# Two token tiles' row sums and norms moved ahead of the first tile's biases on VectorE, in the opening of layer 0's attention

## The chip, the cores and the metric

The kernel runs on one core of a Trainium2 chip. A core has TensorE for matmuls (PE in the profile; its weight loads are PEld), VectorE (DVE), ScalarE (ACT), GpSimd (POOL) and SyncE (SP), which mostly issues DMAs. The engines run their own instruction lists in order and wait for each other by semaphores. The metric is the device time of one launch in microseconds; times in this document are microseconds, counted from the start of the profiled span.

## The reference

Two transformer layers in half-step ("macaron") form on 1024 tokens of width 512, all in float32:

```python
x = L0_attn_hidden_states                      # (1, 1024, 512)
x = x + 0.5 * L0_ffn(layernorm(x))             # 16 experts, top 4, and a shared expert
x = x + L0_attn(layernorm(x))                  # 32 query heads, 8 key/value heads of 16, RoPE, causal
x = x + 0.5 * L0_ffn(layernorm(x))
x = x + 0.5 * L1_ffn(layernorm(x))             # permuted, 16 heads, GELU
x = x + L1_attn(layernorm(x))
x = x + 0.5 * L1_ffn(layernorm(x))
```

The expert layer and the attention, cut to what matters here:

```python
out = einsum('eti,ehi->th', silu(x @ Wg.T) * (x @ Wu.T) * cw, Wd)   # routed part, 4 of 16 experts
out = out + silu(x @ Sg.T) * (x @ Su.T) @ Sd.T                      # shared expert

qkv = einsum('bsh,oh->bso', x, w_qkv) + b_qkv
q, k = rope(q), rope(k)
probs = softmax(where(mask, q @ k.T / 16, min))
out = (probs @ v) @ w_dense.T + b_dense
```

The mask is causal at this length: each query sees all keys up to its own place.

## The kernel before, in words

The 1024 tokens lie in eight tiles of 128 rows. `x_sb` holds all of them in on-chip memory for the whole kernel, one row a partition. The stages follow each other: routing and experts of layer 0, its attention, the same expert layer again, then layer 1.

The expert stage writes its rows, sorted by expert, to a table `y_d` in DRAM. Each token has four rows there. The attention's opening brings them back, and finishes the shared expert for tiles 4 to 7, while it already prepares the first tiles for the scores. The steps of the opening, by the names in the code:

- `moe.fetch(t)` (L869) issues four indirect gathers on GpSimd's queue, which bring the four rows of each token of tile t into buffers `yk`, of which there are eight, for two tiles. `moe.add(t)` (L877) adds them to `x_sb` with four VectorE additions of 128x512.
- `norm_a(t)` (L927) takes the statistics on VectorE (`bn_stats`, `bn_aggr`, an epsilon added) and the power -0.5 on GpSimd (`norm_stats`, L283). `norm_b(t)` (L930) makes the normed rows `xn` with one VectorE instruction.
- `turn(t)` (L933) turns `xn` with four TensorE transposes, and ScalarE copies the result to `xT`.
- `z20` to `z31` (the hidden part of the shared expert) are matmuls with `wsh`, an activation and a VectorE product. `y4` to `y7` (`shared_y`, L524) are the output of the shared expert for tiles 4 to 7: four matmul instructions each, and one VectorE instruction that adds half of it to `x_sb`.
- `project_q(t)` (L943) and `project_kv(t)` (L951) are eight matmul instructions each with `wqkv_sb`, followed by VectorE additions of the bias `bqkv_sb`: one of 128x512 for the queries, two of 128x128 for keys and values.
- `rope_a(t)` and `rope_b(t)` (L966, L976) rotate queries and keys with four VectorE instructions for tiles 0 to 2 and write `aug`. `turn_k` and `turn_q` (L983, L996) turn `aug` with ten TensorE transposes, and ScalarE copies them to `kT` and `qt`.
- `maxima(t, i)` (L1193) computes scores only to find each row's maximum: masks and products on TensorE, four reductions on VectorE. `max_done(t)` (L1056) turns the maxima `nm` and sends them with four SyncE DMAs into a spare row of `qt`, so that the later score matmuls subtract them.
- `moe.collect((4, 5), k)` (L881) issues gathers on GpSimd's queue that add rows of tiles 4 and 5 to `x_sb` in flight. `mid()` loads the shared expert's weights for the second expert layer.

The order is written out by hand. Matmuls are pinned in program order (`pin`, L69). VectorE and GpSimd work goes through a wrapper that ties each instruction to the one before it on that engine (`Ordered`, L89), so the order of the calls at L1201 to L1245 is the order on these engines, within each. All matmul results lie in eight banks of matmul memory that are handed out in turn (`bank`, L123). A bank is written again when its reader is done.

After L1245 a loop over the eight tiles mixes the scores of tile t, the maxima of tile t+1 and the projections of tile t+2.

## Time and profile before

| | us |
|---|---|
| runs, median (lowest to highest of 3) | 1266.63 (1263.77 to 1272.97) |
| the profiled execution | 1270.88 |
| its span from first to last instruction | 1269.2 |

Busy time of the engines in five stretches of the profiled span, with the clock granted to TensorE as a share of full speed:

| stretch, us | what runs | TensorE busy | VectorE busy | clock |
|---|---|---|---|---|
| 290 to 340 | opening of the attention | 42.10 of 50 | 28.74 | 0.93 |
| 340 to 380 | scores of the first tiles | 32.56 of 40 | 21.34 | 0.79 |
| 380 to 700 | the rest of the attention | 313.72 of 320 | 206.62 | 0.98 |
| 700 to 1046 | routing and experts again | 321.81 of 346 | 78.84 | 0.96 |
| 1046 to 1269 | layer 1 | 174.75 of 223 | 106.36 | 0.87 |

How to read the lines of such a profile. A timeline line has the start, the time that the instruction or the group took, the engine, the line of the code (often that of a helper: L82 is every matmul, L85 every transpose, L99 everything that goes through the ordering wrapper), the operation, what is written and read, the shape and the count. In brackets is the time that the engine stood idle before it, and whose end released it. A line of the windows has the window, its length, the busy time of TensorE, its weight loads, VectorE, ScalarE and GpSimd, each with the number of instructions, and then the granted clock, the share of the DMA engines and GB/s.

### The profile page before, as it was taken

Reading aid. Unit: us, or ns where it says so; the run is one execution under the profiler, and the core shown is the slowest. Engines: PE = TensorE matmul, PEld = TensorE weight load, DVE = VectorE, ACT = ScalarE, POOL = GpSimd, SP = SyncE. Lnnn points to the kernel's source line nnn. Section 1 sums busy time; section 2 is a strip of 40 time slices with the busy share of each in tenths; the row PEclk is TensorE's granted clock in tenths of the full one; section 3 lists DMA queues with packets and bytes.
Section 4 is the critical chain, followed back from the end, with each engine's and each line's share of the span. In section 5 each row is a group of like instructions: output and inputs, shape, how many; then the busy total and the mean of one; then the engine's idle time right before and its main releaser. Section 6 shows DMA issues by size and latency. Waiting matters only on the chain. (4 is left out here: it accounts for less than half of the span.)

```text
span 1269.2 us, 18211 instructions
## 1 busy us (share of the span) xinstructions
PE 1158.0 (91%) x6230; PEld 528.4 (42%) x6230; DVE 511.4 (40%) x1172; ACT 451.3 (36%) x868; POOL 307.6 (24%) x377
## 2 busy tenths in 40 slices
PE   8899999997889999999989997899998997697886
PEld 6543333335534444444333335444333336354432
DVE  4711111114566674656587206341111115645631
ACT  4312222221245535363555683112221221431543
POOL 5201112104345522021101010411111107552032
PEclk7999999999979999899989998899999998877998
DMA  6545467524422200000000003546247515630034
GB/s 233 183 158 175 150 215 273 168 92 120 114 34 35 43 1 10 1 10 9 10 1 10 10 1 108 207 153 202 89 142 273 175 52 156 185 122 3 21 119 159
DMA packets 49329, 133.87 MB, mean 105 GB/s; under 512 B 6496, under 2 KB 13408, under 8 KB 45136
## 3 DMA queue, kind: packets, MB, share of 16 engines
q1 hardware_dynamic: 22112, 63.10, 14.4%
q0 software_dynamic: 15152, 47.53, 13.4%
q10 hardware_dynamic: 11968, 22.02, 4.6%
q8 instruction: 52, 0.85, 0.3%
q14 instruction: 45, 0.37, 0.1%
HBM read 276.15 MB, written 34.08 MB: 244 GB/s over the span
## 5 line engine op out<-in xcount | busy, mean ns | idle before, releaser
L82 PE MATMUL ps<-wg,xsT 128*64 128x512 f32 x1120 | 263.3, 612 | 8.5 <-DMA wg<-in_w_exp_dram 6.7
L99 DVE TENSOR_REDUCE nm<-ps 128x1 f32<-128x512 f32 (+5 forms) x360 | 195.2, 599 | 78.3 <-PE ps L82 77.8
L82 PE MATMUL ps<-kT,qt 32*128 32x512 f32 (+3 forms) x768 | 168.8, 536 | 3.5 <-DVE nm L99 3.2
L1098 ACT ACTIVATE pt<-ps 128x512 f32<-128x512 f32 x224 | 119.3, 602 | 126.5 <-PE ps L82 126.1
L82 PE MATMUL ps<-qt,kT 32*128 32x512 f32 x576 | 155.0, 652 | 1.6 <-DMA qt<-nmT 1.1
L747 POOL DMA_INDIRECT xs<-xn_d,src_i x70 | 68.0, 972 | 358.8 <-PE ps L85 316.8
L82 PEld LDWEIGHTS ps<-wg,xsT 128*64 128x64 f32 x1120 | 76.7, 140 | 145.4 <-issue 141.0
L82 PE MATMUL ps<-wd,zT 128*64 128x512 f32 x560 | 133.3, 593 | 1.0 <-DVE zT L99 1.0
L99 DVE TENSOR_TENSOR z<-sg,ps 128x256 f32<-128x256 f32 x70 | 29.4, 421 | 249.5 <-ACT sg L99 249.5
L99 ACT ACTIVATE sg<-ps 128x256 f32<-128x256 f32 x70 | 26.8, 384 | 259.4 <-PE ps L82 259.4
L808 ACT ACTIVATE y<-ps,w_row 128x512 f32<-128x512 f32 x70 | 48.1, 687 | 105.5 <-PE ps L82 56.6
L99 POOL TENSOR_TENSOR rstd<-rstd,mhalf 128x1 f32<-128x1 f32 x48 | 28.7, 599 | 229.3 <-DVE rstd L99 225.0
L82 PEld LDWEIGHTS ps<-kT,qt 32*128 32x128 f32 x768 | 63.7, 187 | 45.1 <-DVE nm L99 14.9
L99 POOL TENSOR_SCALAR_AFFINE_SELECT pt<-pt 128x512 f32<-128x512 f32 x64 | 41.1, 653 | 165.0 <-ACT pt L1102 154.2
L82 PE MATMUL ps<-pt,va 128*32 128x512 f32 x576 | 80.4, 624 | 0.0
L99 POOL DMA_INDIRECT yk<-y_d,row_i x48 | 50.5, 1052 | 95.4 <-SPq L859 82.4
L82 PEld LDWEIGHTS ps<-wd,zT 128*64 128x64 f32 x560 | 40.8, 137 | 78.8 <-issue 77.3
L82 PEld LDWEIGHTS ps<-qt,kT 32*128 32x128 f32 x576 | 49.9, 188 | 54.3 <-issue 27.1
L99 DVE COPY zT<-ps 128x256 f32<-128x256 f32 x70 | 29.6, 423 | 102.6 <-PE ps L85 102.5
L82 PE MATMUL ps<-xT,wsh 128*128 128x256 f32 x256 | 62.8, 402 | 4.8 <-PEq L859 2.6
L85 PE MATMUL ps<-ident,xn 128*128 128x128 f32 x192 | 35.9, 318 | 33.7 <-DVE xn L99 28.1
L82 PEld LDWEIGHTS ps<-xT,wsh 128*128 128x128 f32 x256 | 50.2, 201 | 15.2 <-ACTq L859 6.6
(238 smaller groups left out, 1413.8 us busy)
## 6 DMA issues: line engine op xcount, KB each, us to landing
wg<-in_w_exp_dram SPq DMA_DIRECT2D x142, 1024.0 KB
wd<-in_w_exp_dram SPq DMA_DIRECT2D x142, 512.0 KB
y_d<-y ACTq DMA_DIRECT2D x70, 256.0 KB
xn_d<-xn SPq DMA_DIRECT2D x16, 256.0 KB
wsh<-in_w_exp_dram SPq DMA_DIRECT2D x2, 1536.0 KB
xd<-xT SPq DMA_DIRECT2D x12, 256.0 KB
y_d<-y ACTq DMA_DIRECT2D x2, 1280.0 KB
out_dram<-xo SPq DMA_DIRECT2D x8, 256.0 KB
```

The lines of the kernel that those rows point to most:

```text
L82: pin(nc.tensor.matmul(dst, lhsT=lhsT, rhs=rhs, start=start, stop=stop))
L85: pin(nc.tensor.transpose(dst, src, ident))
L99: ins = f(*a, **k)
L747: nc.gpsimd.indirect_dma_start(out=xs, out_offset=None, in_=self.xn_d, in_offset=bass.IndirectOffsetOnAxis(ap=self.src_i[:, s : s + 1], ax ...
L808: nc.scalar.activation(y, py, AF.Copy, scale=self.w_row[:, s : s + 1])
L1098: nc.scalar.activation(pt, pas[j], AF.Exp, scale=1.0 / 16.0)
```

## The change

In the hand-written order of the opening, four calls of tile 1 and two of tile 2 stand elsewhere. `moe.add(1)` and `norm_a(1)` come ahead of `y4()` and `project_q(0)`; `norm_b(1)` comes ahead of `project_kv(0)` and the rotation of tile 0; `turn(1)` comes ahead of `y5()`; `moe.add(2)` and `norm_a(2)` come ahead of `project_q(1)`.

```diff
             moe.fetch(2)
             z31()
             turn(0)
-            y4()
-            project_q(0)
             moe.add(1)
             norm_a(1)
             moe.fetch(3)
+            y4()
+            project_q(0)
+            norm_b(1)
             project_kv(0)
+            turn(1)
             rope_a(0)
             rope_b(0)
-            norm_b(1)
             y5()
-            turn(1)
             turn_k(0)
             turn_q(0, 0)
             turn_q(0, 1)
-            project_q(1)
             moe.add(2)
             norm_a(2)
+            project_q(1)
             project_kv(1)
             maxima(0, 0)
             rope_a(1)
```

No instruction is added or removed. In the lists of the two programs VectorE's order differs in these places; TensorE's differs in one, where the four transposes of tile 1's `xn` now stand ahead of the four matmuls of `y5`; those of ScalarE, GpSimd and SyncE are the same.

## The prediction

> **What bounds the kernel now.** I read the page first, then the stretch around the change: TensorE's timeline and waits, VectorE's timeline, GpSimd's timeline, and the granted clock in narrow windows. On the page TensorE carries the span; the chain that ended last runs back only to 1046.7 us, so it says nothing of this stretch, which lies at 290 to 345 us.

> ```profile
> PE 1158.0 (91%) x6230; PEld 528.4 (42%) x6230; DVE 511.4 (40%) x1172; ACT 451.3 (36%) x868; POOL 307.6 (24%) x377
> ```

> TensorE is 91% busy over all, but only 9.65 of 14 us between 313 and 327, at a mean clock of 0.76. From 380 to 700 it is busy 313.72 of 320 us. So time that TensorE gains before 345 should reach the end, unless something behind it waits for a thing that doesn't move.

> TensorE's timeline in the stretch (start, time taken, operation, count; in brackets the idle time before and who ended it):

> ```profile
> 305.69 5.32 PE L82 MATMUL ps<-wqkv_sb,xT 128*128 128x512 f32 x16
> 310.85 1.88 PE L82 MATMUL ps<-wsh,zs 128*128 128x512 f32 x4
> 317.35 1.11 PE L85 MATMUL ps<-ident,xn 128*128 128x128 f32 x4 [4.62 <-DVE xn L99]
> 318.26 2.34 PE L85 MATMUL ps<-ident,aug 128*128 128x128 f32 x10
> 320.39 6.18 PE L82 MATMUL ps<-wqkv_sb,xT 128*128 128x512 f32 x16
> 326.41 1.03 PE L82 MATMUL ps<-cmask,ident_b 128*128 128x512 bf16 x4
> ...
> 344.96 0.66 PE L82 MATMUL ps<-qt,kT 32*128 32x512 f32 x1 [1.12 <-DMA qt<-nmT]
> ```

> The reader is to see the 4.62 us in which TensorE waits for VectorE's normed rows of tile 1 (xn), and that the same sixteen projection matmuls take 5.32 us for tile 0 and 6.18 us for tile 1. VectorE's timeline says why:

> ```profile
> 304.15 0.42 DVE L99 TENSOR_TENSOR zs<-sgs,ps 128x256 f32<-128x256 f32 x1 [0.76 <-ACT sgs L99]
> 305.89 0.69 DVE L99 SCALAR_TENSOR_TENSOR x_sb<-ps,x_sb 128x512 f32<-128x512 f32 x1 [1.32 <-PE ps L82]
> 309.32 0.69 DVE L99 TENSOR_TENSOR qk<-ps,bqkv_sb 128x512 f32<-128x512 f32 x1 [2.74 <-PE ps L82]
> 309.93 2.86 DVE L99 TENSOR_TENSOR x_sb<-x_sb,yk 128x512 f32<-128x512 f32 x4
> ...
> 313.84 0.28 DVE L99 TENSOR_TENSOR qk<-ps,bqkv_sb 128x128 f32<-128x128 f32 x1
> ...
> 316.75 0.54 DVE L99 TENSOR_SCALAR xn<-x_sb,mv,rstd 128x512 f32<-128x512 f32 x1
> ...
> 324.88 0.69 DVE L99 TENSOR_TENSOR qk<-ps,bqkv_sb 128x512 f32<-128x512 f32 x1 [6.99 <-PE ps L82]
> ```

> VectorE sits idle for 1.32 + 2.74 us after 304.57, while the sum of tile 1's rows (four adds, 309.93) stands behind the first bias (309.32). From 309.32 it works without a pause to 317.9, then idles 6.99 us while the sum of tile 2's rows waits behind the second bias. In the same place the clock falls:

> ```profile
> 315.00:316.00 1.00, 0.00 (x0) 0.00 (x0) 0.94 (x2) 0.00 (x0) 0.99 (x1) 0.64 0.00 0
> 316.00:317.00 1.00, 0.00 (x0) 0.00 (x0) 0.99 (x2) 0.00 (x0) 0.71 (x1) 0.50 0.23 45
> 322.00:323.00 1.00, 1.00 (x4) 0.42 (x3) 0.00 (x0) 0.00 (x0) 0.00 (x0) 0.95 0.14 53
> ```

> The third number from the right is the granted clock: full until 315.3, half until 322.1.

> **The change, step by step.** It removes and adds no instruction. ACT, POOL and SP keep their order; TensorE only swaps tile 1's four transposes with tile 4's shared output. VectorE has three moves.

> *Tile 1's rows and norm sums go ahead of tile 4's shared sum and the first bias.* The block (4 adds, statistics, aggregate, epsilon) takes 309.93 to 313.84, that is 3.91 us. It can start at 304.5 and end at 308.4. Its rows are there: their four gathers are issued at 296.26 to 300.01 and the trace gives 3.3 to 3.8 us from issue to landing, so the last lands by 303.8. Tile 4's shared sum slips from 305.9 to about 308.4; nobody waits for it, since its bank is next wanted by the projection of tile 1, after 315. The first bias waits for its matmuls (309.29) and stays at 309.32. The block thus costs nothing: TensorE's projection hides it. If that cover were gone it would cost its 3.91 us.

> *Tile 1's norm goes ahead of the key and value biases.* GpSimd's power needs 0.56 us after 308.5 and sits behind gathers that end at 307.7. So xn runs from 309.9 to 310.5, while TensorE works on the key and value projection until 311.0. Its four transposes (0.44 us at full clock, by the spacing of tile 0's) follow directly. The 4.62 us wait goes; what is late next is the rotated tile (aug). From the key bias to its end is 313.84 to 316.83, 3.0 us; starting at 311.05 it ends at 314.05, against 316.83. TensorE does the swapped transposes and tile 4's output until 313.2, then idles 0.9 us instead of 4.62.

> *Tile 2's rows go ahead of the second bias.* They start after tile 5's shared sum, at 314.6, and end at 318.5 (gathers issued by 306.75, landed by 310.6). The second bias has its matmuls at 318.8, so again TensorE hides the block.

> TensorE from there: ten aug transposes at 314.1, 1.08 us; sixteen matmuls, 5.16 us by tile 0's row (305.69 to 310.85); the masks begin at 320.35 instead of 326.41. Of these 6.06 us, 3.25 come from the earlier start, 0.44 from the transposes moved under cover, and 2.4 from the clock (317.35 to 326.41 is 9.06 us for work of 6.68 at full clock). The maxima add 1.2: before, the first maximum reduction began at 329.79, held up by tile 2's adds; now it follows its matmuls, 2.06 us for masks and products plus the drain, at 322.55. That is 7.25 us earlier. From this reduction to the projection of tile 2 (339.70) the order is unchanged and VectorE sets it: two sets of reductions, rotation, aug, xn. So that projection starts 7.25 us earlier, too.

> One wait behind it is not in this chain: the 1.12 us for the row maxima (nmT) to land at 344.96. They share the DMA engines with the shared weights (issued 335.09, after tile 7's output, so 7 us earlier now) and with four accumulating gathers. These follow tile 2's power on POOL, from 329.56 to about 318.6, hence 11 us earlier. They are queued on POOL behind tile 3's row gathers, which move up as well (314.76 to about 309.4). Less collides, so this wait is worth 0 to 1.12 us; no row shows it alone; I take 0.5.

> Sum: 7.25 + 0.5 = **7.8 us faster**. The profiled execution took 1270.88 us (span 1269.2), so one like it would take 1263.1. That execution lies 4.2 us above the median of the runs, 1266.63; I forecast the median, **1258.8 us**, 0.6% faster.

> [...] POOL issues its gathers of tile 2 at 302.94 to 307.70, and tile 1's adds would now run beside them. Before, the adds of tile 0 (298.10 to 300.97) ran beside issues of 0.94 and 0.95 us, no longer than the issues with VectorE idle. [...]

> **Rivals.**
> *The clock still falls.* In the new order TensorE runs transposes at 311.0, idles near 313.2 and runs transposes again to 315.2. If transposes didn't count as work, 2.0 us in a row would look idle, where 2.6 us sufficed at 312.7. It would cost the 2.4 us again: 1261.2 us. Against it: from 335.06 to 339.70 TensorE ran nothing but transposes, 4.6 us, and the clock is 1.00 in every window there. So 8%. [...]

> *The gain is given back.* A wait behind 345 us that doesn't hang on TensorE or VectorE would swallow it: about 1266.6 us. For it: at 358 to 364.5 TensorE waits again for VectorE (2.07 and 4.06 us) and runs at half clock to 376.7. Against it: VectorE's work there hangs on TensorE's scores of the same tile, so it moves along. 8%.

> *The clock's later falls land better.* The half-clock stretch at 359.7 to 376.7 costs some 5 us, and moving the work against the clock's steps can shorten or lengthen it by 2 to 3 us; the same holds for later falls. Together with 7.8 it might pass 12.7 us: about 1253 us. 9%.

> *Slower: tile 1's rows are not there.* VectorE works in order, so if a gather of tile 1 landed late, tile 4's shared sum, the first bias, xn and the rotation would all stand behind its add. From that add to aug's end is 0.7 + 1.1 + 0.6 + 0.6 + 0.5 + 3.0 = 6.5 us. It decides from a landing at 310.3, where aug is as late as before; a landing at 314 makes the kernel 4 us slower, 1270.6 us. The slowest landing in this stretch, 10.3 us after issue with the shared weights on the queues, would come just at 310.3. 3%.

> **Numbers.** The forecast gets 72%. The three runs spread from 2.9 below to 6.3 above their median, and 1% (12.7 us) is about what a measurement of this kernel tells from no change. The range holds the forecast, the falling clock, the full loss of the gain and most of the better clock: 1250 to 1267. Faster by over 1%: 9% and 4% from the forecast's own spread; slower by over 1%: 3% from the last rival and the spread; else within 1%.

> **What would show it.** VectorE's four adds start near 304.5 with no DMA wait; xn of tile 1 ends before TensorE's key and value matmuls do; TensorE's 4.62 us wait is replaced by one under 1 us on aug; the clock is 1.00 throughout 310 to 325; tile 2's projection starts near 332.4. I would be wrong if the clock falls at 315 nevertheless, if VectorE waits for rows, or if the scores of tile 0 don't start some 7 us earlier.

## The result, and the profile after

| | before | changed |
|---|---|---|
| runs, median (lowest to highest) | 1269.80 (1263.77 to 1275.38, 4 runs) | 1255.43 (1252.54 to 1261.19, 4 runs) |
| the profiled execution | 1270.88 | 1256.04 |
| its span | 1269.2 | 1254.3 |

The ratio of the runs is 0.9884, with a 95% interval of 0.9844 to 0.9923: the kernel is 1.2% faster, somewhere between 0.8 and 1.6%. With one more run, the median of the kernel before went from 1266.63 to 1269.80.

TensorE's total in the page of the changed kernel, then its timeline in the same stretch (start, time taken, operation, count, idle time before and who ended it):

```profile
PE 1152.2 (92%) x6230; PEld 525.7 (42%) x6230; DVE 512.0 (41%) x1172; ACT 451.8 (36%) x868; POOL 307.7 (25%) x377
```

```profile
305.63 5.32 PE L82 MATMUL ps<-wqkv_sb,xT 128*128 128x512 f32 x16
310.79 0.60 PE L85 MATMUL ps<-ident,xn 128*128 128x128 f32 x4
311.23 1.88 PE L82 MATMUL ps<-wsh,zs 128*128 128x512 f32 x4
314.11 1.28 PE L85 MATMUL ps<-ident,aug 128*128 128x128 f32 x10 [1.00 <-issue]
315.23 5.33 PE L82 MATMUL ps<-wqkv_sb,xT 128*128 128x512 f32 x16
320.39 1.03 PE L82 MATMUL ps<-cmask,ident_b 128*128 128x512 bf16 x4
...
332.51 3.70 PE L82 MATMUL ps<-wqkv_sb,xT 128*128 128x512 f32 x8 [0.78 <-ACT xT L99]
336.05 0.59 PE L82 MATMUL ps<-cmask,ident_b 128*128 128x512 bf16 x2
336.57 0.69 PE L82 MATMUL ps<-qt,kT 32*128 32x512 f32 x1
```

The wait of 4.62 us on tile 1's normed rows is gone. What is left is a wait of 1.00 us ahead of the rotated tile (the line names no releaser; VectorE's last instruction for `aug` ends at 314.01). The second set of projections takes 5.33 us, as long as the first. The scores of tile 0 (336.57) follow their masks without the wait of 1.12 us on the row maxima. VectorE's timeline of the changed kernel shows the blocks in their new places:

```profile
303.93 2.87 DVE L99 TENSOR_TENSOR x_sb<-x_sb,yk 128x512 f32<-128x512 f32 x4
...
307.85 0.68 DVE L99 SCALAR_TENSOR_TENSOR x_sb<-ps,x_sb 128x512 f32<-128x512 f32 x1
309.27 0.69 DVE L99 TENSOR_TENSOR qk<-ps,bqkv_sb 128x512 f32<-128x512 f32 x1 [0.74 <-PE ps L82]
309.88 0.54 DVE L99 TENSOR_SCALAR xn<-x_sb,mv,rstd 128x512 f32<-128x512 f32 x1
310.99 0.29 DVE L99 TENSOR_TENSOR qk<-ps,bqkv_sb 128x128 f32<-128x128 f32 x1 [0.58 <-PE ps L82]
...
314.52 2.86 DVE L99 TENSOR_TENSOR x_sb<-x_sb,yk 128x512 f32<-128x512 f32 x4
...
322.59 2.48 DVE L99 TENSOR_REDUCE nm<-ps 128x4 f32<-128x512 f32 x4 [1.51 <-PE ps L82]
```

The window of 313 to 327, in which TensorE was busy 9.65 of 14 us at a clock of 0.76, now reads 13.00 us at full clock (the columns are window, length, busy time of TensorE, its weight loads, VectorE, ScalarE, GpSimd, then the clock, the share of the DMA engines and GB/s):

```profile
313.00:327.00 14.00, 13.00 (x105) 7.92 (x105) 10.87 (x22) 1.45 (x3) 6.54 (x6) 1.00 0.45 81
```

Where the 14.9 us between the two profiled spans lie, from the start times of the same TensorE work in both traces:

| stretch | before | changed | difference |
|---|---|---|---|
| up to tile 0's projection | 305.69 | 305.63 | -0.06 |
| from there to tile 2's projection | 34.01 | 26.88 | -7.13 |
| to the first scores | 5.26 | 4.06 | -1.20 |
| to tile 3's key and value projection | 35.63 | 34.28 | -1.35 |
| to the last output projection of the attention | 387.64 | 383.75 | -3.89 |
| to the end | 500.94 | 499.69 | -1.25 |

The first 8.3 us are what the change was reckoned to do. The other 6.5 us stand where nothing was changed, and the later experiments ask where they come from.

### The profile page after: what moved, and what is told of

Its sections match the earlier page's. It is cut to its first block, busy times and chain, and to the rows that moved or that the text cites. A ratio compares the mean times of both kernels' runs of the same rounds, so it can differ in the third digit from the quotient of the medians.

```text
span 1254.3 us, 18211 instructions
## 1 busy us (share of the span) xinstructions
PE 1152.2 (92%) x6230; PEld 525.7 (42%) x6230; DVE 512.0 (41%) x1172; ACT 451.8 (36%) x868; POOL 307.7 (25%) x377
## 3 DMA queue, kind: packets, MB, share of 16 engines
q1 hardware_dynamic: 22112, 63.10, 14.8%
## 5 line engine op out<-in xcount | busy, mean ns | idle before, releaser
L82 PE MATMUL ps<-wg,xsT 128*64 128x512 f32 x1120 | 263.4, 613 | 9.1 <-DMA wg<-in_w_exp_dram 6.8
L99 DVE TENSOR_REDUCE nm<-ps 128x1 f32<-128x512 f32 (+5 forms) x360 | 195.4, 601 | 77.5 <-PE ps L82 77.0
L82 PE MATMUL ps<-kT,qt 32*128 32x512 f32 (+3 forms) x768 | 167.9, 533 | 3.5 <-DVE nm L99 3.3
L82 PE MATMUL ps<-qt,kT 32*128 32x512 f32 x576 | 155.3, 658 | 0.5 <-DVE nm L99 0.4
L82 PEld LDWEIGHTS ps<-wg,xsT 128*64 128x64 f32 x1120 | 76.8, 140 | 146.3 <-issue 143.8
L82 PE MATMUL ps<-wd,zT 128*64 128x512 f32 x560 | 132.4, 593 | 1.0 <-DVE zT L99 1.0
L99 DVE TENSOR_TENSOR z<-sg,ps 128x256 f32<-128x256 f32 x70 | 29.5, 421 | 250.4 <-ACT sg L99 250.4
L99 ACT ACTIVATE sg<-ps 128x256 f32<-128x256 f32 x70 | 26.9, 384 | 260.1 <-PE ps L82 260.1
L99 POOL TENSOR_TENSOR rstd<-rstd,mhalf 128x1 f32<-128x1 f32 x48 | 29.2, 609 | 217.2 <-DVE rstd L99 211.1
L82 PEld LDWEIGHTS ps<-kT,qt 32*128 32x128 f32 x768 | 63.1, 185 | 45.2 <-DVE nm L99 14.9
L99 POOL TENSOR_SCALAR_AFFINE_SELECT pt<-pt 128x512 f32<-128x512 f32 x64 | 41.0, 651 | 166.3 <-ACT pt L1102 155.9
L82 PE MATMUL ps<-pt,va 128*32 128x512 f32 x576 | 78.4, 610 | 0.0
L99 POOL DMA_INDIRECT yk<-y_d,row_i x48 | 50.1, 1044 | 95.4 <-SPq L859 82.4
L82 PEld LDWEIGHTS ps<-wd,zT 128*64 128x64 f32 x560 | 40.5, 137 | 78.7 <-issue 76.6
L82 PEld LDWEIGHTS ps<-qt,kT 32*128 32x128 f32 x576 | 49.6, 189 | 52.4 <-issue 24.0
L99 DVE COPY zT<-ps 128x256 f32<-128x256 f32 x70 | 29.6, 424 | 100.8 <-PE ps L85 100.6
L82 PE MATMUL ps<-xT,wsh 128*128 128x256 f32 x256 | 61.9, 398 | 4.7 <-PEq L859 2.5
L85 PE MATMUL ps<-ident,xn 128*128 128x128 f32 x192 | 36.4, 321 | 25.7 <-DVE xn L99 21.5
L82 PEld LDWEIGHTS ps<-xT,wsh 128*128 128x128 f32 x256 | 49.7, 199 | 15.1 <-ACTq L859 6.5
```

Source lines behind the costliest of these rows:

```text
L82: pin(nc.tensor.matmul(dst, lhsT=lhsT, rhs=rhs, start=start, stop=stop))
L85: pin(nc.tensor.transpose(dst, src, ident))
L99: ins = f(*a, **k)
```

## The experiments

In all of them "the stretch" is the time from the start of tile 0's projection to that of tile 2: 34.01 and 34.32 us in two profiles of the kernel before, 26.88 and 26.87 in two of the changed kernel.

**One tile's moves alone.** `tile1_alone` is the changed kernel with tile 2's two calls put back:

```diff
-            moe.add(2)
-            norm_a(2)
             project_q(1)
+            moe.add(2)
+            norm_a(2)
```

> Tile 1's four moves are made, tile 2's rows and norm sums stay behind the second bias. If VectorE's order is what counts, as the prediction has it: TensorE's 4.62 us wait goes, the clock stays full between 305 and 325, and from the start of tile 0's projection to tile 1's masks it is 14.7 us as in the changed kernel (20.7 before). The reductions of the first maxima start late again, some 1.2 us later after the masks than in the changed kernel, because tile 2's adds stand in front of them. From the start of tile 0's projection to that of tile 2 it is about 28.1 us (26.9 changed, 34.0 before). If instead the clock alone gave the gain, tile 2's place would not matter: 26.9 us.

Measured: from tile 0's projection to tile 1's masks 14.80 us (14.7 expected), and the stretch 28.47 us (28.1 expected). Some 0.4 of that is the half clock under its last four transposes (1.06 us for 0.60). So tile 2's place is worth about 1.2 us of the stretch, and tile 1's the rest. Behind the stretch came something unexpected: the projection of tile 2 took 6.18 us instead of 3.70, because the clock fell at 331.7. TensorE's timeline of this kernel:

```profile
328.92 0.28 PE L85 MATMUL ps<-ident,nm 128*32 128x128 f32 x1 [0.46 <-DVE nm L99]
330.61 1.35 PE L85 MATMUL ps<-ident,aug 128*128 128x128 f32 x10 [1.40 <-DVE aug L99]
331.75 1.06 PE L85 MATMUL ps<-ident,xn 128*128 128x128 f32 x4
333.49 6.18 PE L82 MATMUL ps<-wqkv_sb,xT 128*128 128x512 f32 x8 [0.68 <-ACT xT L99]
```

`tile2_alone` is the kernel before with only those two calls moved ahead.

> Only tile 2's rows and norm sums are moved ahead of the second bias; tile 1's stay behind the first. If VectorE's order is what counts: the 4.62 us wait on tile 1's normed rows stays, the clock falls to half for some 3.4 to 6.8 us after it, and only the 1.2 us ahead of the first reductions are gained: about 32.8 us from the start of tile 0's projection to that of tile 2 (34.0 before, 26.9 changed). If the two moves were worth about the same, it would be near 30.5 us.

Measured: the stretch 32.65 us (32.8 expected), the 4.62 us wait and the fall of the clock at 314.9 still there. It also lacks the wait on the row maxima: from tile 2's projection to the first scores it is 4.07 us, as in the changed kernel. GpSimd's rows fit a link between that wait and tile 2's move. Its power, and the accumulating gathers behind it, come right after tile 3's gathers:

```profile
321.82 0.56 POOL L99 TENSOR_TENSOR rstd<-rstd,mhalf 128x1 f32<-128x1 f32 x1 [1.11 <-DVE rstd L99]
322.56 1.64 POOL L99 DMA_INDIRECT x_sb<-y_d,row_i  x1 [0.18 <-issue]
```

Before, the first of these gathers was issued at 330.30, 9.4 us ahead of tile 2's projection; here it is 15.7 us ahead, so they have 6 us more to land before the row maxima are sent.

**The clock alone.** `clock_kept` is the kernel before, with matmuls of zeros in the place of the wait:

```diff
             y5()
+            fill_ps = bank().rearrange("p (n q) -> p n q", q=P)
+            for _ in range(18):
+                mm(fill_ps, zero, zero.unsqueeze(1).to_broadcast([P, 4, P]))
             turn(1)
```

> The kernel before, with 18 matmuls of zeros put on TensorE (into a bank that nobody reads) where it waits for tile 1's normed rows; they add work but no result depends on them. They last some 3.9 us, inside the 4.62 us wait. If the clock falls because TensorE idles: no fall near 315, tile 1's sixteen projection matmuls take 5.3 us instead of 6.2 and the ten transposes of the rotated tile 1.3 instead of 2.3; from the start of tile 0's projection to tile 2's it is 34.0 - 2.4 = 31.6 us. If the clock's fall has another cause, it falls all the same and the stretch stays at 34 us. The difference between 31.6 and the changed kernel's 26.9 is what the order on VectorE gives without the clock: 4.7 us.

Measured, TensorE's timeline of this kernel:

```profile
311.84 4.05 PE L82 MATMUL ps<-zero 128*128 128x512 bf16 x18
316.62 0.66 PE L85 MATMUL ps<-ident,xn 128*128 128x128 f32 x4 [0.73 <-DVE xn L99]
317.40 1.28 PE L85 MATMUL ps<-ident,aug 128*128 128x128 f32 x10
318.52 5.33 PE L82 MATMUL ps<-wqkv_sb,xT 128*128 128x512 f32 x16
...
334.53 2.04 PE L85 MATMUL ps<-ident,aug 128*128 128x128 f32 x10 [1.46 <-DVE aug L99]
336.37 1.06 PE L85 MATMUL ps<-ident,xn 128*128 128x128 f32 x4
338.10 5.48 PE L82 MATMUL ps<-wqkv_sb,xT 128*128 128x512 f32 x8 [0.68 <-ACT xT L99]
```

The fall at 315 is gone and the transposes and projections take their full-clock times, as expected: the idle time causes this fall. At the masks 2.0 us are gained. But the clock falls at 334.9 instead, in the next place with waits, and at tile 2's projection only 0.9 us are left (33.14 us against 31.6 expected). The kernel took 1268.1 us beside 1268.35 for the kernel before, in one run of each, so no gain shows. With the clock kept by work without use the stretch is 0.9 us shorter, with the new order 7.1: the order on VectorE is what shortens it.

**The norm's place.** `norm_late` is the changed kernel with `norm_b(1)` and `turn(1)` where they were:

```diff
-            norm_b(1)
             project_kv(0)
-            turn(1)
             rope_a(0)
             rope_b(0)
+            norm_b(1)
             y5()
+            turn(1)
```

> The changed kernel, but with tile 1's norm behind tile 0's rotation and its transposes behind tile 5's output, as before; the rows and sums stay moved. If the rows and sums are the main part: TensorE waits about 1.7 us for the normed rows after tile 5's output, and has the four transposes (0.44 us) behind that wait, so the stretch from the start of tile 0's projection to tile 2's is 0.6 to 0.8 us longer than in the changed kernel, about 27.6 us, with no fall of the clock near 315. If the place of the norm is what frees TensorE, the wait stays over 3 us and the stretch is 30 us or more.

Measured: the wait is 1.90 us (1.7 expected), but the stretch is 29.70 us, not 27.6, because the clock fell at 315.9 all the same:

```profile
311.36 1.88 PE L82 MATMUL ps<-wsh,zs 128*128 128x512 f32 x4
315.13 0.66 PE L85 MATMUL ps<-ident,xn 128*128 128x128 f32 x4 [1.90 <-DVE xn L99]
315.88 2.35 PE L85 MATMUL ps<-ident,aug 128*128 128x128 f32 x10
```

Of the 2.8 us that the stretch is longer than in the changed kernel, 1.7 are the half clock under the ten transposes and the projections behind them. The other 1.1 are the norm's place (0.6 to 0.8 expected).

One run was taken of each of these four kernels, beside one of 1268.35 us of the kernel before: 1263.98 (`tile1_alone`), 1259.57 (`tile2_alone`), 1268.1 (`clock_kept`) and 1268.5 us (`norm_late`). Runs of the kernel before lie up to 11.6 us apart, so single runs say little, and these don't follow the stretch: `norm_late` has a stretch 4.3 us shorter than the kernel before and is no faster.

```profile
311.87:315.28 3.41, 0.86 (x2) 1.00 0.00 0
335.76:339.17 3.41, 1.77 (x15) 1.00 0.92 258
356.24:359.65 3.41, 1.75 (x8) 1.00 0.77 117
```

```profile
328.28:331.69 3.41, 1.55 (x12) 1.00 0.87 186
```

```profile
312.49:315.90 3.41, 1.42 (x7) 1.00 0.65 181
```

After 0.86, 1.42, 1.55 and 1.75 us of work the clock fell at the step's end; after 1.77 it stayed. The 1.75 us are products of the scores, which use 32 rows of TensorE (32*128 in the lines); the other steps have none of these. In the kernel before and the changed kernel between 290 and 700 us, and in `tile1_alone` and `norm_late` between 304 and 384 us, every step at full clock without such products fell when it was up to 1.55 us busy and stayed from 1.77 us on. So for this work the limit lay between 1.55 and 1.77 of 3.41 us, and whether a given wait makes the fall depends on where it lies in the grid: around the same transposes the step was 1.77 us busy in the kernel before and 1.55 in `tile1_alone`. For steps with score products busy time doesn't tell: in `rope_early` one of 2.33 us fell, and steps that were busy nearly throughout fell, too, as is shown below. The place of the steps against the start of the span differs from profile to profile: the first begins 1.25 us after it in the kernel before, 0.55 in the changed kernel, and by the steps above 0.6 in `tile1_alone` and 1.9 in `norm_late`.

**Both kernels again.** Each was run once more on one chip, with its own profile.

> The changed kernel once more, with its own profile. The traces differ by 14.8 us, of which the stretch up to tile 2's scores gives 8.3. If the rest came from where the clock's later falls happen to land, this profile has another number of falls than the first (between 340 and 700 us the kernel before had three, 30.7 us in all, and the changed kernel two, 20.5), and the five rounds give a ratio nearer 0.993 than 0.988. If the rest belongs to the change, the falls stay as in the first profile and the ratio is again 0.988.

Measured: 1254.40 us (6 runs), a ratio of 0.9894 (0.985 to 0.9938) to the kernel before. Between 340 and 700 us the profile has 17.1 us at half clock, in two falls.

> The kernel before against itself: a ratio of 1.000 within some 0.004, and a second profile. If the later falls of the clock are luck, their number between 340 and 700 us differs from the first profile's three by one or more, or their lengths do, and the span moves with them by 2 to 5 us. If they belong to the order of the work, the same three falls stand at the same work.

Measured: 1270.99 us (12 runs), a ratio of 1.0007 (0.9981 to 1.0033). Between 340 and 700 the profile has 34.1 us at half clock, in five falls (30.7 in three before). By the expectation this number of falls speaks for chance: the order of the work alone doesn't fix where the clock falls. The gain repeats all the same, and so does the difference in the clock. The runs show it without a profile, too. The traces of the two kernels have no clock but 1.00 and 0.50, so time x (1 - mean clock) x 2 is the time at half clock, and its mean is 126.0 us in the six runs of the changed kernel and 143.4 in the twelve of the kernel before. That is 17.4 us less, worth at most half of it, 8.7 us. The removed fall at 315 is 6.8 of the 17.4.

**The idea carried on.** `tile3_early` is the changed kernel with tile 3's rows and norm sums moved from the first round of scores into the opening:

```diff
             mid()
+            moe.add(3)
+            norm_a(3)
             project_q(2)
...
-                    enter.append(lambda: moe.add(3))
+                    enter.append(nothing)
...
-                    enter.append(lambda: norm_a(t + 3))
+                    enter.append(lambda: norm_a(t + 3) if t else None)
```

> The changed kernel with the same idea carried on: tile 3's rows and norm sums go from the first round of scores, where TensorE waits for VectorE, to the 4.54 us in which VectorE idles ahead of tile 2's query bias. If VectorE's order is what counts: the block of 3.91 us is hidden there, the rotated tile 2 is ready 2.9 us earlier, TensorE's wait for it falls from 4.18 to about 1.3 us, and the kernel gains 2.9 us over the changed one; up to 4 us more where the half-clock stretch behind that wait shortens or goes. Ratio to the kernel before 0.985 to 0.99. If the gaps are only moved elsewhere, the time is that of the changed kernel.

Measured: the wait falls as expected, from 4.18 to 1.40 us (first the timeline of the changed kernel, then of this one):

```profile
356.01 2.37 PE L85 MATMUL ps<-ident,aug 128*128 128x128 f32 x10 [4.18 <-DVE aug L99]
```

```profile
354.09 2.24 PE L85 MATMUL ps<-ident,aug 128*128 128x128 f32 x10 [1.40 <-DVE aug L99]
```

From tile 0's projection to tile 3's key and value projection it takes 60.97 us, against 65.22 and 62.82 in the two profiles of the changed kernel. Yet the median is 1256.66 us (ratio 0.9900, 0.9853 to 0.9947) beside 1254.40: no gain shows. With six runs of each, from 1249.64 to 1261.21 and from 1252.64 to 1260.10, one of 2 us could be hidden.

`rope_early` has, in addition, tile 1's rotation ahead of the first reductions:

```diff
-            maxima(0, 0)
             rope_a(1)
-            maxima(0, 1)
             rope_b(1)
+            maxima(0, 0)
+            maxima(0, 1)
```

> The kernel with tile 3's rows early, and in addition tile 1's rotation ahead of the first maxima's reductions, where VectorE idles 1.5 us. If VectorE sets the stretch between the reductions and tile 2's projection: that projection starts about 1.3 us earlier after the masks, and the kernel gains 1.3 us more. If the reductions of the first maxima set it (their result goes through two transfers), it is 0.9 us later for them and nothing is gained.

Measured: from the masks to tile 2's projection 10.64 instead of 12.07 us, so 1.4 us (1.3 expected), but then the scores wait 0.75 us for the row maxima, which gives back half. The median is 1257.55 us (ratio 0.9898, 0.985 to 0.9946). Neither kernel beats the changed one.

**Where the work stands in the clock's grid.** In the traces so far, the rest of the attention took 383.7 to 392.7 us for the same work, from tile 3's key and value projection to the last output projection. Between the kernel before (387.6) and the changed kernel (383.7) the difference is mostly one fall of the clock, some 137 us after that projection. Two kernels move the work behind it by a bit of work without use, put at the start of tile 2's scores (5 matmuls into the kernel before, 10 into the changed one):

```diff
                     now[0] += 1
+                    if t == 2 and k == 0:
+                        fill_ps = bank().rearrange("p (n q) -> p n q", q=P)
+                        for _ in range(5):
+                            mm(fill_ps, zero, zero.unsqueeze(1).to_broadcast([P, 4, P]))
```

> The kernel before, with 5 matmuls of zeros (1.1 us, into a bank that nobody reads) on TensorE at the start of tile 2's scores, some 10 us after the key and value projection of tile 3. The theory: whether the clock falls again some 137 us after that projection depends on where the work stands in the clock's steps of 3.41 us. In the traces so far it fell there where the projection began 0.3 or 0.45 us after a step (the kernel before), or where the work reached it at 2.6 to 3.0, and not where it stood at 1.0 to 1.7 (the changed kernel, tile 1 alone, tile 2 alone). Moved by 1.1 us the kernel before stands at 1.4 to 1.8: the fall at 137 us goes, the stretch from that projection to the last output projection is 384 to 385 us although work was added (387.7 and 390.0 in the two profiles before), and the kernel is 2 to 4 us faster than before. If the fall belongs to the order of the work, it stays and the stretch is about 389 us. If it is chance of the run, nothing follows from the shift.

> The changed kernel, with 10 matmuls of zeros (2.2 us, into a bank that nobody reads) on TensorE at the start of tile 2's scores. By the theory of the clock's steps the work moves from 1.0 to 1.7 us after a step to 3.2 to 3.9, that is to -0.2 to 0.5, where the kernel before stood: the fall some 137 us after tile 3's key and value projection returns, and the stretch from there to the last output projection is about 390 us (383.7 and 384.3 in the two profiles of the changed kernel), 2.2 of it the added work; the kernel is some 6 us slower than the changed one, 1261 us. If the extra gain belongs to the changed order itself, only the 2.2 us are lost: 386.2 us and 1257 us.

> The kernel before with the 5 added matmuls once more, for a second profile: by the clock's steps no fall some 137 us after tile 3's key and value projection, and 384 to 385 us from there to the last output projection, if the projection stands at 0.3 to 0.7 us after a step again; elsewhere the fall follows where it stands.

> The changed kernel with the 10 added matmuls once more, for a second profile: by the clock's steps a fall some 137 us after tile 3's key and value projection and about 390 us from there to the last output projection, if the projection stands at 1.0 to 1.7 us after a step again; elsewhere the fall follows where it stands.

Measured, with the place of the projection in the grid (time since the last step) and what was added behind it:

| kernel | place + added, us | half clock 130 to 145 us later | stretch of the attention, us |
|---|---|---|---|
| before | 0.45 | 6.8 | 387.6 |
| before_again | 0.73 (1.9 late on the way) | 3.4 | 390.0 |
| clock_kept | 0.31 | 6.8 | 387.7 |
| changed | 1.67 | none | 383.7 |
| after_again | 1.03 | none | 384.3 |
| tile1_alone | 1.67 | none | 383.7 |
| tile2_alone | 1.14 | none | 384.2 |
| norm_late | 1.17 (1.5 late on the way) | 3.4 | 392.7 |
| tile3_early | 2.98 | 3.4 | 385.7 |
| rope_early | 2.30 (3.3 late on the way) | 6.8, in two | 391.9 |
| before_plus1 | 1.09 + 1.1 | none | 384.4 |
| before_plus1b | 0.42 + 1.1 | none | 384.9 |
| after_plus2 | 1.70 + 2.2 = 0.5 after the next step | 6.8 | 389.7 |
| after_plus2b | 0.18 + 2.2 | none | 385.3 |

"Late on the way" is how much later the first output projection came than in the other kernels without added work, which have it some 41.5 us after tile 3's projection. The windows of 500 to 530 us show the fall in one figure, the clock, third from the right. First the kernel before, then `before_plus1`, the changed kernel, and `after_plus2`:

```profile
500.00:530.00 30.00, 29.64 (x128) 13.92 (x125) 18.95 (x35) 12.04 (x22) 4.75 (x7) 0.89 0.02 7
```

```profile
500.00:530.00 30.00, 29.64 (x148) 12.90 (x147) 18.98 (x35) 9.60 (x18) 3.70 (x6) 1.00 0.00 1
```

```profile
500.00:530.00 30.00, 29.64 (x173) 13.14 (x172) 22.02 (x46) 8.93 (x17) 4.49 (x5) 1.00 0.00 1
```

```profile
500.00:530.00 30.00, 29.64 (x148) 12.80 (x146) 18.96 (x38) 7.91 (x14) 2.21 (x3) 0.89 0.00 1
```

TensorE is busy 29.64 of 30 us in all four, so this fall isn't made by a wait, as the one at 315 is. The step ahead of it in the kernel before (the columns are those of the single steps above) holds score products but for 0.19 us of its time:

```profile
513.26:516.67 3.41, 3.05 (x12) 1.00 0.00 0
```

In `norm_late` and `tile3_early` the step ahead of it is busy for the whole 3.41 us. What in this work lets the clock fall was not tested.

Work that stood 1.0 to 2.4 us after a step met no fall there; work at 0.3 to 0.5 or 2.6 to 3.0 did. `before_plus1b` and `after_plus2` met the condition of their expectations and did what it says. `before_plus1` and `after_plus2b` began elsewhere than expected, and followed where they stood. `rope_early` speaks against so simple a rule: it arrives at about 2.2 and falls twice. The column adds the work at its full length, though, and the traces show that less of it arrives: at the first output projection the 5 matmuls have delayed the work by 0.7 and 0.9 us, the 10 by 1.8 and 1.6. Taken where that output projection starts, the place in the grid parts all 14 profiles: 1.64 to 2.36 us after a step in the seven without the fall, 2.74 to 3.19 or 0.13 to 0.93 in the seven with it, `rope_early` with 2.74 among them. This rule is read from the same profiles, and no run was made to test it.

In time, the kernel before with 1.1 us of useless work is faster than without: 1267.64 us over 12 runs beside 1271.18, a ratio of 0.9969 (0.9942 to 0.9996). The changed kernel with 2.2 us added has 1263.89 us over 11 runs, a ratio of 0.9934 (0.9903 to 0.9965), against 0.9894 (0.985 to 0.9938) without; the medians differ as expected, but these two intervals overlap. The single runs behind the second profiles took 1275.22 (`before_plus1b`) and 1260.92 us (`after_plus2b`). The clocks of the runs bear out the first kernel and not the second. The time at half clock, reckoned as above, has a mean of 145.8 us in the 22 runs of the kernel before beside them and of 135.9 in those of `before_plus1`. In those of `after_plus2` it is 129.3, that is 16.5 less than before, nearly as in the changed kernel (17.4 less). So on the mean the added work did not bring time at half clock back, and why `after_plus2` loses more than its 2.2 us stays open.

## Why the prediction came out as it did

**The opening: right, in nearly every figure.** VectorE's adds of tile 1 start at 303.93 without a wait (304.5 reckoned). The first bias stays, at 309.27. xn runs from 309.88 (309.9). The rotated tile lets TensorE go at 314.11 after 1.00 us of idling (314.1, 0.9). The masks begin 5.96 us earlier (6.06), the first reduction at 322.59 (322.55), and tile 2's projection at 332.51 (332.4). The steps between were tested one by one: tile 1's moves and tile 2's (`tile1_alone`, `tile2_alone`), and the norm's place, which is worth 1.1 us and 1.7 more by the fall of the clock (`norm_late`).

**The wait on the row maxima: right in kind, mis-sized.** It was put at 0.5 us, with 1.12 as its end. It went wholly, and the stretch behind tile 2's projection became 1.20 us shorter. `tile2_alone` fits the reason that was given: with tile 2's move alone the accumulating gathers start 6 us earlier against the rest, and the wait is gone. That they alone made it was not tried. `tile1_alone`, where they start late as before, can't tell: its scores don't wait either, but its projection of tile 2 took 2.5 us longer, at half clock, and gave the row maxima that much more time.

**POOL beside VectorE's adds.** The prediction's rows left one out: a third gather issue beside tile 0's adds, at 300.01, took 1.05 us. In the changed kernel the issues of tile 2 took 1.10, 0.96, 1.11 and 1.14 us, and the adds (303.93 to 306.80) ran beside the last three. So they were longer by 0.4 us or so in all, one of them with no add beside it, and none by the 0.7 us of an add; the power then waited 0.40 us for VectorE and not for them, and nothing came of it.

**The falling clock as a rival: rejected on one lucky row.** The prediction took the 4.6 us of transposes at 335 to 339.7 as evidence that such a place can't bring the clock down. TensorE was idle for 2.64 of these 4.64 us. The step there was 1.77 of 3.41 us busy and stayed; in `tile1_alone` and `clock_kept` the same instructions lay otherwise in the grid and the clock fell, at 331.7 behind a step of 1.55 us and at 334.9. The rival did not happen in the changed kernel, whose step at 311.2 to 314.6 is 2.41 us busy. But the row proved less than was made of it. Whether transposes count as work can be answered better from single steps: steps with nothing but transposes kept the clock, with 1.77 us of them in the kernel before (335.76 to 339.17) and 1.91 in the changed kernel (328.23 to 331.64), and in `after_plus2` the step from 357.12 to 360.53, with 3.15 us of transposes, brought it from half back to full. So in these traces they count.

**The sum: too small by about 7 us.** The forecast was 7.8 us faster; the medians of the result differ by 14.4, the spans differ by 14.9, and the medians of the repeat by 16.6 (1270.99 and 1254.40). The term that was mis-sized is the clock behind the changed stretch. The prediction gave it to a rival at 9% ("the clock's later falls land better", about 1253 us) and left it out of the forecast's sum. That the forecast of 1258.8 us still lies within 3.4 us of the measured 1255.43 is partly luck: the median that it started from, 1266.63 of three runs, was itself 3 to 4 us low (1269.80 with a fourth, 1270.99 in the repeat), and hid half of the gain that was missing. The runs show that the clock differs between these two kernels: 17.4 us less at half clock, of which the sum held only the 6.8 at 315. The account nearly closes: 8.3 us up to the first scores, of which 2.4 are the clock's, leaves 5.9 of order and transfers; at most 8.7 from the clock makes 14.6. That these later falls follow from the work's place in the grid, and not from the new order as such, is likely for the largest of them, by the 14 profiles and by the runs of `before_plus1`, but not shown: the runs of `after_plus2` became slower without more time at half clock. For the falls in the experts and layer 1 (1.25 us between the profiles) it was not tested. Why the two kernels come to different places in the grid is only partly answered: profiles of the same kernel scatter (0.42 to 1.09 before, 0.18 to 1.70 changed), though the mean times at half clock of their runs differ (125.6 and 126.0 us in the two sets of the changed kernel, 143.4 and 145.8 in two of the kernel before).

**The other rivals.** The gain was not given back in this kernel. In `tile3_early` and `rope_early`, which reach tile 3's projection another 1.9 to 5.0 us sooner after tile 0's, no such gain shows at the end. Falls of the clock may have taken it: some 137 us behind tile 3's projection their profiles have one and two, the changed kernel's none. But the mean time at half clock of their runs, 125.2 and 128.6 us, is hardly above the changed kernel's 126.0, so where that gain went stays open. The rows of tile 1 were there in time; the last rival had no case.

## What to carry to other kernels

A block on an in-order engine belongs where that engine idles while the bound engine has work in hand; the cost of a wait is read from what is queued behind it, and here two timelines gave most of the new start times within 0.1 us or so. Count a wait on TensorE together with the clock behind it (here 4.62 us of waiting had 6.8 us at half clock behind it): keep each step of the clock's grid of 3.41 us busier than the 1.55 us that let it fall here (1.77 kept it), don't expect that to be enough where the work is products of 32 rows (behind 3.05 us, nearly all of them such products, it fell in the kernel before), and don't trust one trace in which a half-idle place kept its clock. Where gains of a few us are at stake, look at the mean clock of several runs besides the time: 1.1 us of work without use moved the median of this kernel by 3.5.

## What was not expected of the hardware

- A wait of 1.90 us brought the clock down for a step (`norm_late`); a step of 3.41 us with 1.55 us of work without score products did (`tile1_alone`), one with 1.77 did not (the kernel before).
- The clock also fell where TensorE was busy nearly throughout, behind steps that were busy for 3.05 of 3.41 us in the kernel before, all but 0.19 of it with score products of 32 rows, and for the whole 3.41 in `norm_late` and `tile3_early`.
- Busy time doesn't tell when the clock comes back, either: in `norm_late` a step of 3.24 us, most of it transposes, brought it back (360.28 to 363.69), but in the kernel before it stayed at half through two steps that were 3.24 and 3.42 us busy, mostly with the 32-row score products, and rose after one of full projections. The columns are those of the single steps above:

```profile
366.48:369.89 3.41, 3.24 (x14) 0.50 0.02 5
369.89:373.31 3.42, 3.42 (x15) 0.50 0.62 87
```

- 1.1 us of added matmuls made the kernel before faster by 0.3% (0.9942 to 0.9996).
